# The opening of a two-layer fp32 kernel: unread products, an early table load, another order of transfers

## The chip, the cores and the metric

The kernel runs on one core of a Trainium2 chip. The metric is the time of the program on the device, in microseconds; a smaller time is better. The kernel before took 775.93 us, the median of three runs (774.78 to 776.19). The profile shows one more execution.

The engines are named as in the profile: PE (TensorE; PEld is its weight load), DVE (VectorE), ACT (ScalarE), POOL (GpSimd) and SP (SyncE, which here only issues transfers). ACT issues transfers too.

## What is computed

Two transformer layers on `x` of shape (4, 512, 256), all in fp32. Only the beginning of the first layer bears on the change:

```python
xn = _layernorm(x)                         # (x - mean) / sqrt(var + 1e-5)
x = x + _L0_attn_ref(xn, ...) + _L0_ffn_ref(xn, ...)
# inside the attention
h_in = _rmsnorm(xn, norm1_w)               # norm1_w * xn * rsqrt(mean(xn^2) + 1e-6)
v = h_in @ wv
i_pre = _soft_cap(h_in @ w_ig + b_ig)
f_pre = _soft_cap(h_in @ w_fg + b_fg)
# inside the feed-forward network
router_logits = xn @ Wr.T
```

The attention is a gated linear attention (mLSTM) with eight heads, followed by a gated MLP; the feed-forward network has eight low-rank experts of which two are chosen per token. The second layer has a softmax attention and an MLP with a 2-of-4 sparsification. The output is `x` after both layers.

## The kernel before

**Tiling.** The 512 positions are cut into four tiles `j` of 128; a tile holds the 128 positions of all four batches, as `x_sb[j]` of shape [128, 4, 256], so `b` below is one of four rows of a tile. Each tile is normalised, transposed on PE (128x128 at a time), and multiplied with the weights. All work goes out on in-order engines.

**What sets the order.** The kernel has a planner: a class `Clock` that keeps an estimated time for each engine and each buffer, and a class `Flow` that runs generators ("streams") as their due times come. The estimates decide in which order instructions are written into each engine's queue; once built, the order is fixed. So an instruction added at the front changes estimates, and can change the order later. PSUM has eight banks, all handed out by `mm_ps`; a bank whose last estimated user is PE counts as not free.

**Transfers.** They are issued by SP and ACT in program order, into SBUF tiles. At most eight were outstanding at a time in this trace: the ninth issue, on whichever of the two engines, waits until an earlier one has landed. All weights of both halves of the first layer are issued at the start, from `load_x(0)` (L342) to L382; they take until about 36 us to land.

**The opening.** `load_x(0)` fetches the four rows of the first tile in four transfers, three on SP and row 1 on ACT. Then ACT fetches the four parts of `wvg` (values, two gates, router: 256 + 8 + 8 + 8 columns), SP fetches `norm1_w` after the first of these, ACT the two gate biases. `first_front` (L528) is the first tile's front: ACT multiplies the 272 columns of `wvg` that belong to the attention by `norm1_w` (L538; the router's 8 columns stay as they are); for each row, DVE takes the statistics (`bn_stats`, `bn_aggr`), Pool adds the epsilon and takes the power -0.5, DVE normalises (`normed`, L540), PE transposes into `pt`, ACT copies into `xnT`, and PE multiplies by `wvg` into `vp` (`values`, L516). The row that is normalised is one behind the row whose statistics are taken, and the product is one behind that. After it `choice` picks the experts, while PE goes on with the low-rank products `lp`, with `q_ps`, `k_ps`, and, after `spread`, with `chunk`, the experts' products.

A matrix product of two fp32 operands takes two passes on PE, so one `mm` over 256 contracted elements shows as four records; a transpose shows as one.

Of the kernel before, what the change touches and what calls it, by code (L numbers as in the profile page):

```python
# [9 lines left out]
AF = mybir.ActivationFunctionType  # L10
ALU = mybir.AluOpType
AX = mybir.AxisListType

P = 128
B, S, D = 4, 512, 256
NJ = S // P
KD = D // P
H, DQK, DV = 8, 16, 32
# [4 lines left out]
E, R, K_TOP = 8, 16, 2  # L23
# [9 lines left out]
def layers_kernel(ctx: ExitStack, tc: tile.TileContext, io: dict, out: bass.AP):  # L33
    nc = tc.nc
    x_d = io["x"]

    const = ctx.enter_context(tc.tile_pool(name="const", bufs=1))
# [7 lines left out]
    def n_of(ap):  # L45
        n = 1
        for m in ap.shape[1:]:
            n *= m
        return n

    class Clock:
# [36 lines left out]
        def room(self, n):  # L88

            return sorted(self.bank_free(i) for i in range(BANKS))[n - 1]  # L90


        def part(self, ap):
# [86 lines left out]
        def dma(self, out, in_, us, kind="sp"):  # L180
            start = max(self.free[kind], self.ready(out, reads=True, but="dma"),
                        self.ready(in_)) + 0.5
            self.free[kind] = start
            self.free["dma"] = max(start, self.free["dma"]) + us
            end = self.free["dma"] + 2.0
            for ap, w, r in ((out, end, 0.0), (in_, 0.0, end)):
                self.known(ap.tensor.name).append((*self.part(ap), w, r, "dma"))

    clock = Clock()

    def new(pool, shape, tag, bufs=None, dtype=F32):
        count[0] += 1
        kw = {} if bufs is None else {"bufs": bufs}
        t = pool.tile(shape, dtype, tag=tag, name=f"{tag}_{count[0]}", **kw)
        clock.ring(t, (id(pool), tag), bufs or (2 if tag in ("xn", "xnT") else 1))
        return t

    def mm_ps(name):
        count[0] += 1
        t = psum.tile([P, 512], F32, tag="mm", bufs=BANKS, name=f"{name}_{count[0]}")  # L200
        clock.take_bank(t)
        return t

    class InOrder:
# [15 lines left out]
    pe, dve, act, pool = (InOrder(e, k) for e, k in (  # L220
        (nc.tensor, "pe"), (nc.vector, "dve"), (nc.scalar, "act"), (nc.gpsimd, "pool")))
# [71 lines left out]
    def mm(out, lhsT, rhs, start, stop, at_once=1, **kw):  # L293
        array = (lhsT.shape[0], n_of(lhsT))
        us = 2 * max(0.107, n_of(rhs) * 0.00084) / at_once + 0.1 * (array != clock.array)
        clock.array = array
        clock.issue("pe", "matmul", (out, lhsT, rhs), {}, us)
        pe.matmul(out, lhsT, rhs, start=start, stop=stop, **kw)

    def transpose(out, in_, eye):  # L300
        array = (in_.shape[0], n_of(in_))
        us = 0.11 + 0.1 * (array != clock.array)
        clock.array = array
        clock.issue("pe", "transpose", (out, in_, eye), {}, us)
        pe.transpose(out, in_, eye)
# [6 lines left out]
    def load(t, src, by="sp"):  # L312
        dma(t, src, n_of(t) * t.shape[0] * 4 / 0.3e6, by)
        return t
# [6 lines left out]
            "p (k n) -> p k n", n=n)  # L321
        return load(t, d.rearrange("(k p) n -> p k n", p=P), by)

    def column(name):
        t = new(const, [P, KD], name)
        return load(t, io[name].rearrange("(k p) -> p k", p=P))

    x_sb = []

    def load_x(j):  # L330

        t = new(xres, [P, B, D], f"x{j}")
        x_sb.append(t)
        src = x_d[:, j * P : (j + 1) * P, :].rearrange("b p d -> p b d")
        if j:
            load(t, src)
        else:
            for b in range(B):
                load(t[:, b, :], src[:, b, :], ("sp", "act", "sp", "sp")[b])


    load_x(0)  # L342
    V = D + 2 * H + E
    wvg = new(wts, [P, KD, V], "wvg")
    at = 0
    for name, n in (("wv", D), ("w_ig", H), ("w_fg", H), ("WrT", E)):
        load(wvg[:, :, at : at + n], io[name].rearrange("(k p) n -> p k n", p=P), "act")
        at += n
        if at == D:
            norm1_c = column("norm1_w")  # L350
    gate_b = new(const, [P, 2 * H], "gate_b")
    load(gate_b[:, 0:H], io["b_ig"].partition_broadcast(P), "act")
    load(gate_b[:, H : 2 * H], io["b_fg"].partition_broadcast(P), "act")
# [21 lines left out]
    mh_c = column("mh_w")  # L375
    w_out = weight("w_out", D)
    norm2_c = column("norm2_w")
    w_gate = weight("w_gate", FF)
    w_up = weight("w_up", FF)
    w_down = weight("w_down", D)  # L380
    for j in range(2, NJ):
# [3 lines left out]
    ident = new(const, [P, P], "ident")  # L385
# [15 lines left out]
        out=before, in_=before, pattern=[[1, E], [-1, E]], compare_op=ALU.is_gt,  # L401
# [5 lines left out]
    for base, step in ((0, -2 * DQK), (2 * DQK - 1, 2 * DQK)):  # L407
        nc.gpsimd.affine_select(
            out=own_pair, in_=own_pair, pattern=[[step, H // 2]], compare_op=ALU.is_ge,
            fill=0.0, base=base, channel_multiplier=1 if step < 0 else -1)  # L410
    def inv_sqrt(o, i):
        n = i.shape[1]
        pool.tensor_tensor(out=o, in0=i, in1=mhalf[:, 0:n], op=ALU.pow)
# [58 lines left out]
    with ExitStack() as l0:  # L472
# [8 lines left out]
        def cols_of(i):  # L481
            return slice(i * P, (i + 1) * P)
# [19 lines left out]
        def front_tiles(j):  # L502
            xns[j] = new(both, [P, B, D], "xn")

            rrs[j] = new(sm, [P, 4, B], "rr", 2)
            vas[j] = new(wk0, [P, B, H, DV + 1], "va", 2), new(sm, [P, B, 2 * H], "gz", 2)
            return xns[j], rrs[j], *vas[j], new(both, [P, KD, S], "xnT"), new(sm, [P, B, E], "pr")

        def rms_of(rr, ms, va):

            dve.tensor_tensor(rr[:, 1, :], rr[:, 0, :], rr[:, 0, :], ALU.mult)
            dve.tensor_scalar(rr[:, 2, :], rr[:, 0, :], 0.5, None, ALU.mult)
            dve.tensor_tensor(ms, ms, rr[:, 0, :], ALU.mult)
            dve.tensor_copy(va[:, :, :, DV], rr[:, 0, :].unsqueeze(2).to_broadcast([P, B, H]))

        def values(xnT, b):  # L516
            vp = mm_ps("vp")
            for k in range(KD):
                mm(vp[:, 0:V], xnT[:, k, cols_of(b)], wvg[:, k, :], start=(k == 0),
                   stop=(k == KD - 1))  # L520
            return vp

        def values_read(vp, b, rr, va, gz):
            dve.scalar_tensor_tensor(
                gz[:, b, :], vp[:, D : D + 2 * H], rr[:, 0, b : b + 1], gate_b, ALU.mult, ALU.add)
            act.mul(va[:, b, :, 0:DV], by_head(vp[:, 0:D]), rr[:, 1, b : b + 1])

        def first_front():  # L528

            x = x_sb[0]  # L530
            xn, rr, va, gz, xnT, pr = front_tiles(0)
            stats = new(both, [P, B, 6], "stats", 2)
            mv = new(both, [P, B, 2], "mv", 2)
            rstd = new(both, [P, 2, B], "rstd2")

            for k in range(KD):
                mine = wvg[:, k, 0 : D + 2 * H]
                act.mul(mine, mine, norm1_c[:, k : k + 1])  # L538

            def normed(b):  # L540
                dve.tensor_scalar(
                    xn[:, b, :], x[:, b, :], mv[:, b, 0:1], rstd[:, 1, b : b + 1], ALU.subtract,
                    ALU.mult)
                pt = mm_ps("pt")
                for k in range(KD):
                    transpose(pt[:, k * P : (k + 1) * P], xn[:, b, k * P : (k + 1) * P], ident)
                act.copy(xnT[:, :, cols_of(b)], pt[:, 0 : KD * P].rearrange(
                    "p (k t) -> p k t", k=KD))

            vps = []  # L550
            for b in range(B):
                dve.bn_stats(stats[:, b, :], x[:, b, :])
                dve.bn_aggr(mv[:, b, :], stats[:, b, :])
                pool.tensor_scalar(rstd[:, 0, b : b + 1], mv[:, b, 1:2], 1e-5, None, ALU.add)
                inv_sqrt(rstd[:, 1, b : b + 1], rstd[:, 0, b : b + 1])
                if b:
                    normed(b - 1)
                if b > 1:
                    vps.append(values(xnT, b - 2))

            ms = rr[:, 3, :]
            dve.reciprocal(ms, rstd[:, 0, :])
            dve.tensor_tensor(ms, ms, mv[:, :, 1], ALU.mult)
            dve.tensor_scalar(ms, ms, 1e-6, None, ALU.add)
            inv_sqrt(rr[:, 0, :], ms)
            normed(B - 1)
            for b in range(B - 2, B):
                vps.append(values(xnT, b))
            for w in (wq, wk, w_og):
                for k in range(KD):  # L570
                    pool.tensor_scalar(
                        w[:, k, :], w[:, k, :], norm1_c[:, k : k + 1], None, ALU.mult)
            for b in range(B):
                dve.tensor_copy(pr[:, b, :], vps[b][:, D + 2 * H : V])

            def values_of_all():
                rms_of(rr, ms, va)
                for b in range(B):
                    values_read(vps[b], b, rr, va, gz)

            xnTs[0] = xnT
            yield from choice(0, pr, values_of_all)
# [964 lines left out]
```

## Time and profile before

| What | Value |
|---|---|
| runs | 775.93 us, median of 3 (774.78 to 776.19) |
| profiled execution | 776.43 us |
| its span, first to last instruction | 774.6 us |
| PE's share of the span | 99% |
| first record of PE | 5.71 us, `pt` |
| first product with values | 8.72 us, `vp` |
| first `lp` | 16.09 us |
| granted TensorE clock | 1.0 in all 40 slices |

The page cuts the span into 40 slices of 19.4 us; the first slice is the only one with an idle PE worth the name (busy tenths, then the transfers' rate):

```
PE   6999999999999999999999999999999999999998
GB/s 253 282 97 1 1 1 1 110 ...
```

A transfer is shown from its issue; a wait is the idle time of an engine, with the instruction whose end released it. A wait that depends on several things is put down to the last of them. In the timeline, equal instructions that follow one another are drawn together, with their number after an x.

The opening as ACT saw it (start us, us, engine, line, operation, out<-in, number, idle time before and its releaser):

```profile
0.80 0.42 ACTq L309 DMA_DIRECT2D x<-in_x  x1
1.25 0.45 ACTq L309 DMA_DIRECT2D wvg<-in_wv  x1
...
3.55 0.38 ACTq L309 DMA_DIRECT2D wvg<-in_WrT  x1
4.30 0.35 ACTq L309 DMA_DIRECT2D gate_b<-in_b_ig  x1
5.73 0.35 ACTq L309 DMA_DIRECT2D gate_b<-in_b_fg  x1
6.18 1.28 ACT L216 ACT_TABLE_LOAD   x1 [6.18 <-DMA wvg<-in_WrT]
```

The issues take time on ACT's own queue, and instructions that compute stand behind them.

### The profile page before, as it was taken

How to read it: one execution, taken by the hardware profiler on the slowest of the kernel's cores; microseconds unless marked ns; L12 is line 12 of the kernel's file. 1: busy time of each engine (PE TensorE's matmuls, PEld its weight loads, DVE VectorE, ACT ScalarE, POOL GpSimd, SP SyncE). 2: the span in 40 equal slices, each digit the busy share in tenths (PEclk: the TensorE clock that was granted, in tenths of full speed). 3: DMA queues.
4: the chain of work that ended last, by engine and by line, in shares of the span. 5: the costliest groups of instructions: out<-in, count | busy, mean ns of one | idle time of the engine just before them, and what ended most of it. 6: DMA issues, size and time to landing. Idle time of an engine off the chain costs nothing.

```text
span 774.6 us, 9712 instructions
## 1 busy us (share of the span) xinstructions
PE 763.0 (99%) x3782; PEld 516.6 (67%) x3782; DVE 471.4 (61%) x1070; ACT 225.7 (29%) x457; POOL 160.6 (21%) x151
## 2 busy tenths in 40 slices
PE   6999999999999999999999999999999999999998
PEld 3677786766657776765777774747545575754487
DVE  4878647977552878634378534332366984837980
ACT  2334314332212342313134312010344305243310
POOL 5322051321230410140030041000333203333000
PEclk9999999999999999999999999999999999999999
DMA  8830000300000300000030120001000000000000
GB/s 253 282 97 1 1 1 1 110 1 1 1 1 1 110 0 1 2 0 1 1 110 1 56 96 14 1 0 55 0 1 0 0 28 1 0 28 0 0 28 29
DMA packets 18975, 25.44 MB, mean 33 GB/s; under 512 B 2800, under 2 KB 12784, under 8 KB 18928
## 3 DMA queue, kind: packets, MB, share of 16 engines
q1 hardware_dynamic: 17408, 24.39, 9.9%
q8 instruction: 30, 0.49, 0.3%
q10 hardware_dynamic: 1520, 0.43, 0.2%
q14 instruction: 17, 0.14, 0.1%
HBM read 22.65 MB, written 2.16 MB: 32 GB/s over the span
## 4 chain that ended last, share of the span: by engine, by line
PE 98%; DVE 1%; DMA 1%; ACT 0%; issue 0%
PE chunk L216 20%; PE yp L216 18%; PE up L216 14%; PE gp L216 14%; PE acc L216 11%; PE qk_ps L216 4%; PE vp L216 2%; PE pt L216 2%; PE v_ps L216 2%; PE o_ps L216 2%; PE lp L216 2%; PE qk L216 1%; PE hv L216 1%; PE sums L216 1%; PE k_ps L216 1%; PE q_ps L216 1%
## 5 line engine op out<-in xcount | busy, mean ns | idle before, releaser
L216 ACT ACTIVATE sl<-chunk 128x256 f32<-128x256 f32 x132 | 50.6, 384 | 134.5 <-PE chunk L216 118.1
L216 PE MATMUL chunk<-low,lora 128*128 128x256 f32 (+1 forms) x384 | 87.3, 385 | 0.9 <-DVE he_pair L216 0.7
L216 PE MATMUL chunk<-xnT,wguT 128*128 128x256 f32 (+1 forms) x384 | 84.5, 384 | 0.0
L216 PEld LDWEIGHTS chunk<-xnT,wguT 128*128 128x128 f32 (+1 forms) x384 | 63.6, 181 | 23.5 <-issue 11.5
L216 PEld LDWEIGHTS chunk<-low,lora 128*128 128x128 f32 (+1 forms) x384 | 63.0, 181 | 14.9 <-issue 2.1
L216 DVE SCALAR_TENSOR_TENSOR sl<-sl,chunk 128x256 f32<-128x256 f32 x132 | 54.4, 412 | 11.3 <-ACT sl L216 10.7
L216 PE MATMUL gp<-xnT,wguT 128*128 128x512 f32 x128 | 60.2, 592 | 0.0
L216 PE MATMUL up<-featT,w_up 128*128 128x512 f32 x128 | 60.2, 592 | 0.0
L216 PE MATMUL gp<-featT,w_gate 128*128 128x512 f32 x128 | 60.1, 592 | 0.0
L216 PE MATMUL up<-xnT,lora 128*128 128x512 f32 x128 | 60.1, 592 | 0.0
L216 PE MATMUL yp<-w_down,hid 128*128 128x256 f32 x256 | 56.2, 379 | 0.0
L216 PE MATMUL yp<-w_gate,hs 128*128 128x256 f32 x256 | 56.2, 379 | 0.0
L216 PEld LDWEIGHTS yp<-w_down,hid 128*128 128x128 f32 x256 | 48.5, 190 | 8.2 <-issue 1.7
L216 PEld LDWEIGHTS yp<-w_gate,hs 128*128 128x128 f32 x256 | 48.6, 190 | 6.6
L216 DVE SCALAR_TENSOR_TENSOR tmp<-tmp,gp 128x512 f32<-128x512 f32 x32 | 21.9, 685 | 42.8 <-ACT tmp L216 42.8
L216 ACT ACTIVATE tmp<-gp 128x512 f32<-128x512 f32 x32 | 19.1, 597 | 96.7 <-PE gp L216 96.7
L216 PEld LDWEIGHTS up<-xnT,lora 128*128 128x128 f32 x128 | 24.3, 190 | 29.3 <-issue 28.0
L216 PEld LDWEIGHTS up<-featT,w_up 128*128 128x128 f32 x128 | 24.1, 190 | 27.9 <-issue 26.3
L216 PEld LDWEIGHTS gp<-xnT,wguT 128*128 128x128 f32 x128 | 24.0, 190 | 27.8 <-issue 27.0
L216 PEld LDWEIGHTS gp<-featT,w_gate 128*128 128x128 f32 x128 | 24.1, 190 | 27.6 <-issue 27.3
L216 POOL TENSOR_TENSOR pd<-k,q 128x256 f32<-128x256 f32 (+3 forms) x16 | 25.3, 1583 | 81.8 <-ACT k L216 81.8
L216 PE MATMUL acc<-WdT,hid 128*128 128x256 f32 (+1 forms) x192 | 40.9, 386 | 0.0
(211 smaller groups left out, 1192.0 us busy)
## 6 DMA issues: line engine op xcount, KB each, us to landing
ct<-m_dram SPq DMA_DIRECT2D x8, 1024.0 KB, 8.1
x<-in_x SPq DMA_DIRECT2D x3, 512.0 KB, 9.6
out<-x SPq DMA_DIRECT2D x6, 256.0 KB, 2.1
w_gate<-in_w_gate SPq DMA_DIRECT2D x1, 1024.0 KB, 6.7
w_up<-in_w_up SPq DMA_DIRECT2D x1, 1024.0 KB, 7.6
w_down<-in_w_down SPq DMA_DIRECT2D x1, 1024.0 KB, 10.6
wguT<-in_f_gate SPq DMA_DIRECT2D x1, 1024.0 KB, 5.0
lora<-in_f_up SPq DMA_DIRECT2D x1, 1024.0 KB, 5.0
```

Of the source, the lines that this page charges most:

```text
L216: return tc.keep_in_program_order(f(*args, **kw))
```

## The change

- **Transfers.** The first tile comes in three transfers, all on SP: row 0, row 1, rows 2 and 3 together. `norm1_w` is ACT's first transfer, `wv`, `w_ig` and `w_fg` follow on ACT; the router's part `WrT` goes to SP.
- **Table.** A tile of one column is set to zero on DVE, and ACT takes its exponential, after its first four transfers and ahead of the two gate biases. The result is used by nothing. The number of table loads in the program stays the same.
- **Norm weight.** ACT multiplies the 256 value columns of `wvg`; the 16 gate columns of both halves are multiplied on Pool, by one product with a broadcast `norm1_w`.
- **Unread products.** PE multiplies the identity by itself nine times into a bank `idle`, and twice more after the first row's transposes. `let_go` tells the planner that the bank is free.
- **Order in `first_front`.** DVE takes the statistics of rows 0 to 2, and adds the epsilon itself; Pool takes the powers of rows 0 and 1; row 0 is normalised; then come row 3's statistics, Pool's product for the gates, one power for rows 2 and 3, and rows 1 and 2. `values` still runs one row behind.

Further on, the planner writes some instructions in another order. On PE the order is unchanged to the experts' first `acc` products with `he_pair`; from there on single groups of tiles 0 to 2 change places (the second tile's `vp` after two more groups of `chunk`, and its first `qk` directly after `vp`; `spread` of the next tile one group of `acc` later), and the second layer is unchanged. On DVE the subtraction on `ct` stands one pair of operations earlier.

```diff
@@ class Clock
+        def let_go(self, t):
+            self.known(t[:].tensor.name).append((0, 1 << 40, 0.0, self.free["pe"], ""))
@@ load_x
-            for b in range(B):
-                load(t[:, b, :], src[:, b, :], ("sp", "act", "sp", "sp")[b])
-    load_x(0)
+            for b0, b1 in ((0, 1), (1, 2), (2, 4)):
+                load(t[:, b0:b1, :], src[:, b0:b1, :])
@@ weights
-    for name, n in (("wv", D), ("w_ig", H), ("w_fg", H), ("WrT", E)):
-        load(wvg[:, :, at : at + n], io[name].rearrange("(k p) n -> p k n", p=P), "act")
-        at += n
-        if at == D:
-            norm1_c = column("norm1_w")
+    load_x(0)
+    norm1_c = column("norm1_w", "act")
+    into_wvg("wv", 0, "act")
+    into_wvg("w_ig", D, "act")
+    into_wvg("w_fg", D + H, "act")
+    into_wvg("WrT", D + 2 * H, "sp")
+    early = new(const, [P, 1], "early")
+    nc.vector.memset(early, 0.0)
+    nc.scalar.activation(early, early, AF.Exp)
@@ first_front
-                mine = wvg[:, k, 0 : D + 2 * H]
-                act.mul(mine, mine, norm1_c[:, k : k + 1])
+                act.mul(wvg[:, k, 0:D], wvg[:, k, 0:D], norm1_c[:, k : k + 1])
+            idle = mm_ps("idle")
+            def keep_busy(n):
+                for _ in range(n):
+                    mm(idle[:, 0:P], ident, ident, start=True, stop=True)
+            keep_busy(9)
@@ normed, at its end
+                if b == 0:
+                    keep_busy(2)
+                    clock.let_go(idle)
@@ first_front
-            for b in range(B):
+            def statistics(b):
                 dve.bn_stats(stats[:, b, :], x[:, b, :])
                 dve.bn_aggr(mv[:, b, :], stats[:, b, :])
-                pool.tensor_scalar(rstd[:, 0, b : b + 1], mv[:, b, 1:2], 1e-5, None, ALU.add)
+                dve.tensor_scalar(rstd[:, 0, b : b + 1], mv[:, b, 1:2], 1e-5, None, ALU.add)
+            for b in range(B - 1):
+                statistics(b)
+            for b in range(2):
                 inv_sqrt(rstd[:, 1, b : b + 1], rstd[:, 0, b : b + 1])
-                if b:
-                    normed(b - 1)
-                if b > 1:
-                    vps.append(values(xnT, b - 2))
+            normed(0)
+            statistics(B - 1)
+            gates = wvg[:, :, D : D + 2 * H]
+            pool.tensor_tensor(
+                out=gates, in0=gates, in1=norm1_c.unsqueeze(2).to_broadcast([P, KD, 2 * H]),
+                op=ALU.mult)
+            inv_sqrt(rstd[:, 1, 2:B], rstd[:, 0, 2:B])
+            for b in range(1, B - 1):
+                normed(b)
+                vps.append(values(xnT, b - 1))
```

## The prediction

> **What bounds the kernel now.** I read the page first, for the engine that sets the end, then TensorE's waits, then the chain of waits over the first 24 us.
>
> ```profile
> PE 763.0 (99%) x3782; PEld 516.6 (67%) x3782; DVE 471.4 (61%) x1070; ACT 225.7 (29%) x457; POOL 160.6 (21%) x151
> ```
> ```profile
> PE pt L216 <- DVE xn L216: 5.9, 2, 5.7
> PE vp L216 <- ACT xnT L216: 1.4, 1, 1.4
> PE chunk L216 <- DVE he_pair L216: 0.7, 1, 0.7
> PE yp L216 <- ACT oT L216: 0.2, 1, 0.2
> PE chunk L216 <- DVE tmp L216: 0.2, 1, 0.2
> ```
>
> The second view (total us, times, longest) is the whole of TensorE's idle time: 8.5 us, of which 7.3 lie ahead of 8.72 us. After that TensorE is the bound, so a microsecond saved in the opening reaches the end unless a new wait takes it. The chain of waits of the opening (start, us, what):
>
> ```profile
> 0.80 2.72 DMA x<-in_x
> ...
> 3.55 2.64 DMA wvg<-in_WrT
> 6.19 1.28 ACT L216
> ...
> 7.48 0.93 ACT wvg L216 x2
> 8.41 0.27 ACT xnT L216
> ...
> 8.72 2.23 PE vp L216 x4
> 10.96 0.43 PE pt L216 x2
> 11.38 1.87 PE vp L216 x4
> 13.25 0.43 PE pt L216 x2
> 13.68 2.58 PE vp L216 x8
> 16.25 3.43 PE lp L216 x8
> ```
>
> Two things are to be seen. ACT's table load (1.28 us, the line without a tile) and the two scalings of `wvg` stand behind ACT's own transfers, and the first product with values waits for them. And the products before about 15 us are slow: four of `vp` take 1.87 us, 0.467 each, where the chain of the whole span has for the same 16 products in the next tile
>
> ```profile
> 69.25 3.77 PE vp L216 x16
> ```
>
> that is 0.236 each. Transposes show the same halving, 0.213 against 0.109 in `spread` (0.44 for four). The page's granted clock is 1.0 in every slice, so this is another limit than the throttle that this row records. In the order of single products the step changes once, at 14.9 us, 6.1 us after unbroken work began.
>
> **The change, step by step.** Times are from the start of the span; the sum is against the profiled execution, 776.43 us, 0.5 over the median of 775.93.
>
> *Transfers.* Row 1 of `x` moves from ACT's queue to second on SP, rows 2 and 3 become one 256 KB transfer, third on SP, issued at 1.72. The 128 KB pieces took 3.0 us from issue to landing, `wv` (256 KB) 3.5, `AgT` at a busier moment 4.1: landing between 4.7 and 5.8, I take 5.3, just above `wv`'s. `norm1_w` leaves SP and `WrT` joins it, so `wq` and all behind it keep their place; the weights are needed late (`lp` took its `AgT` long landed).
>
> *Rows.* In DVE's queue the statistics of rows 0, 1 and 2 now stand ahead of the first normalised row, so `xn` of row 0 waits for the large transfer. From 5.3: statistics 0.42, aggregate 0.18, the addition that Pool did (0.25) now on DVE at 0.17 as its 128x4 neighbour, with gaps `xn` starts at 6.1, takes 0.41, and the first `pt` starts at 6.56, against 5.71: **0.85 later**. Row 3's statistics follow, `xn` of row 1 ends at 7.57, its `pt` starts at 7.63.
>
> *ACT.* Its first four transfers are out at 2.74; the table load follows at once, to about 4.0, the one-element activation to 4.3. Then `b_ig` and `b_fg`; the latter went out only at 6.07 in this trace and I leave it there. The two scalings (0.93 together) end by 7.0, the copy of the first `xnT` (0.35) by 7.4. Before, the same copy ended at 8.68. The table load is hidden behind the wait for `x`; without that cover it would cost its 1.28.
>
> *Pool.* Two powers of one column (0.58 each) end by 5.6. The 16 gate columns are a shape this trace lacks: above 0.23 (one column) and below 0.6 (`wq`, 128x128, 0.61); both ends lie between the landing of `w_fg` near 6.0 and the last power's input at 7.25, so nothing is added. The power of two columns lies between 0.58 and the 1.19 of four columns: 0.78 by the line through both, ending at 8.05; `xn` of row 2 ends at 8.5, its `pt` is due on PE at 8.78.
>
> *Values.* `pt` of row 1 takes 0.21 at full speed, so the first `vp` starts at 7.84 instead of 8.72. Then 16 products of 0.236 are 3.78, four transposes 0.43: `lp` starts at 12.05 instead of 16.09. **Gain 4.0 us**: 0.9 from the earlier start, 3.1 from the speed.
>
> *The unread products.* Nine of 128x128, two passes each at 0.213, run from `ident` (1.50) to about 5.36; nothing is behind them before 6.56. The two after the first `pt` take 0.43 at full speed or 0.85 slow, and would push the next `pt` from 7.63 to 7.84 at worst.
>
> Whether they buy the speed is the dispute. The row says 6.1 us of unbroken work were needed: 3.84 is too short, a pause of 1.2 follows, and counted from 6.56 the step would come at 12.7. The Trainium skill (TensorE: Matmul & The Clock Gate, "What's actually happening") says that the clock is halved by default and freed after one busy window of about 3.4 us that runs free of the kernel, and falls back after an idle window as long. By it 3.84 us suffice when a window fits, and a pause of 1.2 loses nothing. The same section speaks against counting on it: one kernel showed 6, 11 or 14 slow products by where the window fell. Slow throughout, `vp` starts at 8.27 and needs 16 x 0.467 + 4 x 0.213 = 8.32, to 16.6, less half of what comes after the step: by the row 14.65, by the page 12.05. I take the page: 6.1 is what one whole window costs when another had just begun at 8.72, and the three runs' spread of 1.4 us is near the 1.7 that half a window is worth. No run here shows it.
>
> *Further on.* The order from the first `acc` on is re-planned. DVE reaches the first subtraction on `ct` at 49.86 - 4.0 - 0.84 (one pair of products earlier in its queue) = 45.0, but Pool's select, which waits on a transfer behind all the weights, ends at 45.91: 0.9 us in which DVE's queue stands. The pairs behind it free banks with some 2 us to spare, so most is covered. The first `qk` now directly follows `vp` and waits for ACT's reading of its banks (0.47). Against that, the 0.7 wait for `he_pair` may go, as DVE now makes it ahead of the two additions to `xn`. The bounds are -0.7 and +1.4; I take +0.4.
>
> 776.43 - 4.04 + 0.4 = **772.8**.
>
> **Rivals.**
> *The clock is freed late.* For: the 6.1 us of the row, and that the first stretch is hardly longer than a window. Work from 6.56 is then unbroken, so the step comes between 10 and 12.7, `lp` starts at 13.3 to 14.65: 774.0 to 775.4, 774.7 in the middle.
> *Handed back.* The clock is early, but both waits above reach PE in full: 772.4 + 0.9 + 0.5, and another such wait of about 0.4: 774.2. For it: the `ct` landing doesn't move when PE does. Against: PE had no wait between 8.72 and 118 us.
> *Rows late, slower.* The statistics of row 2 hold every row. If the 256 KB land late, PE pauses over 3.4 us after its unread products, and is slow again: `lp` starts 9.3 us after landing (1.26 to `pt`, then 8.1 for slow work that speeds up 6.1 us later). It decides from a landing at 8.3, where `lp` is 1.5 later than before; at 9.8, as `w_og` (256 KB) took 8.1 us from issue, it is 19.1 and the time 779.8. Against: `w_og` stood behind two 704 KB transfers, this one behind 256 KB.
>
> **How the numbers follow.** A difference of 0.2% (1.55 us) is about what this kernel's runs can tell from no change. Early clock 0.53, late clock 0.27, handed back 0.12, late rows 0.08. Faster means under 774.4: nearly all of the first, half of the second, two thirds of the third, 0.73; no change 0.19; slower 0.08. The range goes from 771.8 (landing at 4.7, nothing handed back) to 775.4 (clock by the row).
>
> **What would show it.** Right: `vp` at 0.236 from its first product, first `vp` at 7.8, `lp` near 12, table load near 2.8, later PE waits near 1 us in all. Wrong: the step of 0.467 in several `vp`, a first `pt` well after 6.6, a PE wait near 45 or 70 us, or `ct` landing later than 43.8.

## The result, and the profile after

The changed kernel takes **774.37 us**, the median of 19 runs (772.95 to 775.32); the kernel before, run beside it, takes 775.82 (19 runs, 774.78 to 776.33). The ratio is 0.9984, 95% interval 0.9978 to 0.9991. So the gain is 1.45 us where 3.1 were predicted: the direction and the range hold, the size is just under half. The profiled execution took 774.77 us (span 773.1) against 776.43 (774.6); between these two the gain is 1.66, where the prediction's own sum, which starts from 776.43, has 3.6.

TensorE's waits after the change (us in total, times, longest), to be held against the five of before:

```profile
PE pt L220 <- DVE xn L220: 1.9, 2, 1.8
PE idle L220 <- POOL ident masks.py:199: 1.5, 1, 1.5
PE yp L220 <- ACT oT L220: 0.2, 1, 0.2
PE chunk L220 <- DVE tmp L220: 0.2, 1, 0.2
PE hv L220 <- DVE ct L220: 0.2, 1, 0.2
```

The idle time is halved, from 8.5 us to 4. The 1.4 for `xnT` and the 0.7 for `he_pair` are gone, and one new wait of 0.2 (`hv` for `ct`) has come. But 1.8 us in one piece still stand ahead of the first `pt`.

The chain of waits of the opening (start, us, what):

```profile
1.72 4.19 DMA x<-in_x
5.91 0.02 issue
5.94 0.44 DVE stats L220
...
6.77 0.36 DVE xn L220
...
8.25 0.60 PE pt L220 x2
8.85 1.93 PE vp L220 x4
10.78 0.43 PE pt L220 x2
11.21 1.30 PE vp L220 x4
12.51 0.22 PE pt L220 x2
12.73 1.89 PE vp L220 x8
14.62 3.43 PE lp L220 x8
```

ACT is gone from it: neither the table load nor a scaling stands there any more, and the 256 KB transfer of rows 2 and 3 has taken their place. Four of `vp` take 1.93 us, then four take 1.30, then eight take 1.89: the old slow step, a mixed group, the full speed. The change of speed falls at 11.8 us.

Engines by stretch of the opening (stretch, its length; busy time and instructions of PE, PEld, DVE, ACT, POOL; PEclk, DMA share, GB/s):

```profile
1.60:4.90 3.30, 3.30 (x16) 3.30 (x17) 1.62 (x7) 1.49 (x2) 1.57 (x8) 1.00 0.85 239
4.90:8.30 3.40, 1.47 (x11) 1.09 (x10) 2.12 (x8) 1.28 (x3) 1.09 (x3) 1.00 0.82 170
8.30:11.80 3.50, 3.50 (x10) 2.65 (x11) 1.31 (x6) 0.74 (x2) 2.48 (x4) 0.51 0.90 306
11.80:15.20 3.40, 3.40 (x15) 2.46 (x15) 0.81 (x6) 0.37 (x1) 2.35 (x5) 1.00 1.04 399
```

Here the profile says outright what the page's 40 slices hide. PEclk is the granted share of TensorE's full clock. The trace has clock records that begin at 4.98 (full), at 8.39 (half) and at 11.80 (full), 3.41 us apart. In the first stretch the unread products fill PE, and the clock is free at its end. In the second PE is busy for 1.47 of 3.40 us, and at its end **the clock is taken back**. In the third PE is full again, at half speed, and at its end the clock returns. Passes of 128 columns follow each other by 0.111 us in the second stretch, where the clock is free, and by 0.213 in the third.

From `lp` on nothing has moved: profiled time less the start of the first `lp` is 776.43 - 16.09 = 760.34 before and 774.77 - 14.45 = 760.32 after. The whole gain lies in the opening, and so does the whole shortfall.

This is one execution. The record has the mean granted clock of each run, and one window of 3.41 us at half speed lowers it to 0.998 over this span (1 - 3.41 x 0.5 / 773.1). Six of the 19 runs read 0.998, at 774.37 to 775.32, the median run among them. The other 13 read 0.999 or 1.000 and lost no whole window behind the first record: two of them are the fastest (772.95 and 773.06), eleven lie at 773.91 to 774.96. Time ahead of the first clock record counts as full in this mean, so a clock that is freed late leaves no mark in it. Late freeing is the likely reason for these eleven, but none of them was profiled.

### The profile page after: what moved, and what is told of

Same layout as the page of the kernel before. It is cut to its first block, busy times and chain, and to the rows that moved or that the text cites. A ratio compares the mean times of both kernels' runs of the same rounds, so it can differ in the third digit from the quotient of the medians.

```text
span 773.1 us, 9758 instructions
## 1 busy us (share of the span) xinstructions
PE 765.8 (99%) x3804; PEld 519.9 (67%) x3804; DVE 471.1 (61%) x1075; ACT 226.1 (29%) x458; POOL 158.6 (21%) x147
## 4 chain that ended last, share of the span: by engine, by line
PE 97%; DVE 1%; DMA 1%; issue 0%; SPq 0%; ACT 0%
PE chunk L220 20%; PE yp L220 18%; PE up L220 14%; PE gp L220 14%; PE acc L220 11%; PE qk_ps L220 4%; PE pt L220 2%; PE vp L220 2%; PE o_ps L220 2%; PE v_ps L220 2%; PE lp L220 2%; PE qk L220 1%; PE k_ps L220 1%; PE q_ps L220 1%; PE hv L220 1%; PE sums L220 1%
```

## The experiments

The theory after the result: the unread products do free the clock, but the pause behind them gives it back for one window of 3.41 us, which costs about 1.7 us (3.41 us of work done at half speed). Its rivals: the unread products are useless, and the gain is that of transfers and table; or the late rows alone are the trouble; or the gain is lost further on; or, in other runs than the profiled one, the clock is freed late.

Results in one table. The first three columns are those of the profiled execution: start of the first `vp`, start of the first `lp`, and the time less the latter. "Freed" is the start of the first clock record.

| Kernel | `vp` | `lp` | rest | freed | median us (runs: lowest to highest) | ratio to before (95%) |
|---|---|---|---|---|---|---|
| before | 8.72 | 16.09 | 760.34 | 14.94 | 775.92 / 775.71 / 775.86, on three chips | 1 |
| changed kernel | 8.64 | 14.45 | 760.32 | 4.98, lost 8.39 to 11.80 | 774.37 (19: 772.95 to 775.32) | 0.9984 (0.9978 to 0.9991) |
| a_no_idle | 8.46 | 13.82 | 760.51 | 10.77 | 774.82 (21: 774.03 to 775.78) | 0.9987 (0.9981 to 0.9994) |
| a_fill | 8.84 | 13.05 | 760.35 | 6.86 | 773.13 (5: 772.83 to 774.20) | 0.9965 (0.9951 to 0.9979) |
| a_split | 7.74 | 12.04 | 760.62 | 4.78 | 772.66 (5: 772.43 to 773.88) | 0.9960 (0.9947 to 0.9972) |
| **a_row01** | 7.65 | 12.15 | 760.33 | 5.06 | **772.48** (5: 772.37 to 772.58) | 0.9954 (0.9942 to 0.9967) |
| b_idle | 8.82 | 13.14 | 760.27 | 7.30 | 773.45 (13: 773.29 to 775.23) | 0.9980 (0.9972 to 0.9988) |
| b_table | 8.02 | 14.84 | 760.25 | 13.12 | 775.06 (13: 774.19 to 775.75) | 0.9992 (0.9984 to 1.0000) |
| c_both | 8.23 | 12.55 | 760.26 | 6.18 | 772.81 (5: 772.73 to 772.92) | 0.9961 (0.9948 to 0.9973) |
| c_row01_cold | 7.54 | 14.52 | 760.41 | 13.01 | 774.48 (11: 773.72 to 775.38) | 0.9984 (0.9976 to 0.9993) |
| best1 | 7.80 | 12.09 | 760.89 | 7.20 | 773.08 (5: 772.98 to 773.46) | 0.9968 (0.9956 to 0.9981) |
| best4 | 8.00 | 12.32 | 761.06 | 6.38 | 773.22 (5: 772.88 to 773.38) | 0.9968 (0.9955 to 0.9980) |
| best6 | 7.16 | 12.08 | 760.65 | 5.64 | 773.62 (7: 772.73 to 773.82) | 0.9971 (0.9959 to 0.9982) |

### Without the unread products

```diff
-            keep_busy(9)
-                if b == 0:
-                    keep_busy(2)
-                    clock.let_go(idle)
```

> The changed kernel without the eleven unread products; everything else as changed. Theory 'lost again' (the products free the clock at about 5 us, the pause ahead of the first row takes it back for one window of 3.4 us): without them TensorE is slow from its first row at about 7.2 until a whole window of work has passed, so every product with values up to 11.5 to 15 us steps 0.467, lp starts at 14.5 to 16, and the median is 774.6 to 775.6, 0.2 to 1.2 above the changed kernel's 774.4. Rival 'products useless' (the earlier table load and the order of the rows made the whole gain): median within 0.2 of 774.4.

774.82, only 0.45 more than the changed kernel: most of what the change gains (1.1 of 1.45 us) comes without a single unread product. The opening's chain shows how:

```profile
7.99 0.68 PE pt L220 x2
8.67 1.87 PE vp L220 x4
10.53 0.40 PE pt L220 x2
10.93 0.94 PE vp L220 x4
```

The step of the first `vp` is slow, and the clock comes at 10.77, in the profiled run. Unbroken work begins at 7.99 instead of 8.72, which is 0.7 of the 1.1. The runs spread over 1.75 us, as those of the kernel before do, which fits a clock that is freed at another point in each run. So the median carries the verdict and not this one profile. The rival "useless" is not refuted by this run alone: as they are placed, the unread products bring 0.45 us, inside the uncertainty of a measurement of this kernel.

### The pause filled

```diff
-            keep_busy(9)
+            keep_busy(15)
-                    keep_busy(2)
+                    keep_busy(4)
```

> The changed kernel with fifteen and four unread products instead of nine and two, so that TensorE's pause ahead of the first row shrinks from 2.0 us to about 0.6 where the clock is freed near 5 us. 'Lost again': no fallback, products with values step 0.236 from the first one, lp starts near 12.7 instead of 14.45, the median is 772.8 to 773.4; where the clock is freed late, fifteen slow products (6.4 us) end at 7.9 and delay the first row by 0.7, so single runs may be at 775. 'Products useless' or 'rows alone bind': median 774.2 to 775.

773.13. The longer run of unread products ended at 7.67 by the chain and held the first `pt` back from 7.18 to 7.50; the first `vp` is 0.2 later than in the changed kernel, and `lp` is 1.4 earlier all the same, since every `vp` runs at 0.236. So the late rows alone are not what cost most: with them just as late and more unread products, 1.24 us of the loss come back. The edit does two things, though: it fills the pause, and it makes the unbroken work longer, so that the clock is also freed early more often. It does not tell the two apart.

### Rows 2 and 3 in two transfers

```diff
-            for b0, b1 in ((0, 1), (1, 2), (2, 4)):
+            for b0, b1 in ((0, 1), (1, 2), (2, 3), (3, 4)):
```

> The changed kernel with rows 2 and 3 of the first tile as two transfers of 128 KB. If the 256 KB transfer (landed at 5.91, 4.19 from issue) is what made the rows late, the statistics of row 2 start 0.5 to 0.7 earlier, near 5.3, the first pt near 6.55, lp 0.6 earlier by that alone, median 773.6 to 774.1, and the pause of 1.3 us left may or may not take the clock back. If the landing is set by the bytes ahead of it on both queues, not by its size: start at 5.7 to 5.9, median 774.2 to 774.5.

772.66. Row 2 landed at 5.12 instead of 5.91, the first `pt` began at 6.36, and the clock that was freed at 4.78 stayed. Of the 2.41 us by which `lp` is earlier than in the changed kernel, 0.90 are the earlier first `vp` and 1.51 the speed behind it: the edit mends two things at once, and in this profile the clock is the larger. The median lies below the expected 773.6 to 774.1, which left open whether the clock would be kept. One of the five runs took 773.88, with no window lost (its mean clock reads 1.000); it was not profiled.

### Rows 0 and 1 normalised first

```diff
-            for b in range(B - 1):
-                statistics(b)
             for b in range(2):
+                statistics(b)
                 inv_sqrt(rstd[:, 1, b : b + 1], rstd[:, 0, b : b + 1])
-            normed(0)
-            statistics(B - 1)
+            for b in range(2):
+                normed(b)
+            for b in range(2, B):
+                statistics(b)
...
             for b in range(1, B - 1):
-                normed(b)
+                if b > 1:
+                    normed(b)
```

> The changed kernel with rows 0 and 1 normalised and transposed before the statistics of rows 2 and 3, so DVE's queue no longer holds them behind the large transfer. 'Rows late': the first pt starts near 5.3, right behind the unread products, the second by 6.0; the first product with values is then bound by the scaling of the value weights on ACT (ends 7.5) and starts near 7.6 instead of 8.64; the pause is now 1.5 us between the second pt and that product. Lp 0.9 to 1.1 earlier if the clock is the same as in the changed kernel, median 773.3 to 773.9. If DVE's queue doesn't bind the start of the values: median within 0.2 of 774.4.

**772.48, the lowest median of all that was run**, with all five runs within 0.21 us. The expected 773.3 to 773.9 supposed the clock of the changed kernel; here it was kept. PE's timeline (start, us, engine, line, operation, out<-in, number, idle time before and its releaser), first of the changed kernel:

```profile
1.52 3.90 PE L220 MATMUL idle<-ident 128*128 128x128 f32 x18 [1.52 <-POOL ident masks.py:199]
7.18 0.44 PE L220 MATMUL pt<-ident,xn 128*128 128x128 f32 x2 [1.76 <-DVE xn L220]
7.46 0.61 PE L220 MATMUL idle<-ident 128*128 128x128 f32 x4
8.25 0.60 PE L220 MATMUL pt<-ident,xn 128*128 128x128 f32 x2 [0.18 <-DVE xn L220]
8.64 2.14 PE L220 MATMUL vp<-wvg,xnT 128*128 128x280 f32 x4
```

and of this version:

```profile
1.52 3.95 PE L220 MATMUL idle<-ident 128*128 128x128 f32 x18 [1.52 <-POOL ident masks.py:199]
5.31 0.38 PE L220 MATMUL pt<-ident,xn 128*128 128x128 f32 x2
5.53 0.61 PE L220 MATMUL idle<-ident 128*128 128x128 f32 x4
6.11 0.44 PE L220 MATMUL pt<-ident,xn 128*128 128x128 f32 x2
7.65 1.18 PE L220 MATMUL vp<-wvg,xnT 128*128 128x280 f32 x4 [1.10 <-ACT xnT L220]
```

The unread products now run straight into the first transposes, and unbroken work lasts from 1.52 to 6.55 instead of 5.43. A pause remains (1.10 us ahead of `vp`), but the window in which it falls is still mostly busy, and the four `vp` take 1.18 us instead of 2.14:

```profile
5.00:8.40 3.40, 2.30 (x15) 1.83 (x15) 1.99 (x9) 1.44 (x4) 1.54 (x3) 1.00 0.84 172
8.40:11.80 3.40, 3.40 (x17) 2.48 (x16) 1.51 (x8) 0.75 (x2) 2.47 (x4) 1.00 0.91 290
```

A window with 2.30 of 3.40 us busy kept the clock, where one with 1.47 of 3.40 lost it.

### That version without the unread products

The edit of a_row01 and that of a_no_idle together.

> The fastest version so far (the changed kernel with rows 0 and 1 normalised first, 772.48) without the unread products; order of the other products as there. It asks what the freed clock is worth where nothing else holds the values. Theory: vp starts near 7.7 as with them, but at 0.467, the step comes one whole window after work became dense, between 10.5 and 13.5, so lp starts at 13.3 to 14.5 instead of 12.15 and the time is 773.6 to 774.8, spread over 1 us or more by where the window falls. Rival (transposes at 5.3 already start the window, so the unread products are worth little here): 772.5 to 773.0.

774.48, and 1.7 us of spread is back. In the profile `vp` starts as early as with the unread products (7.54), the clock is freed at 13.01, and `lp` starts 2.4 us later. So the same unread products that bring 0.45 us in the changed kernel bring **2.0 us** once the rows follow them without a gap. That refutes "useless".

### Unread products alone, on the kernel before

```diff
+            keep_busy(9)
...
+                if b == 0:
+                    keep_busy(2)
+                    clock.let_go(idle)
```

> The kernel before with the unread products alone: nine ahead of the first transposes and two behind them; transfers, table load, order of rows and order of products on TensorE stay as before. It asks what the unread products are worth where the loads stay. TensorE then works from 1.5 to about 5.3, pauses 0.4 or less before the first pt at 5.7 and has a pause of about 1 us before the first vp at 8.7, a shorter one than the 2.0 us that lost the clock in the changed kernel. Theory (a window of 3.4 us with over half of it busy keeps the freed clock): vp at 0.236 from 8.7 on, lp starts near 13 instead of 16.1, time 772.8 to 773.6. Rival (clock lost again in the pause): some vp at 0.467 between 8.7 and 12, lp near 14.7, 774.3 to 774.8. Rival (unread products do nothing by themselves, the gain comes from loads and table): 775.6 to 776.2.

Ratio 0.9980: about what the whole change gains, with the transfers, the table load and the order of all other products as they were. The single runs fall into two groups that are 1.7 us apart: seven at 773.29 to 773.45, six at 774.78 to 775.23, with nothing between. The profiled run (773.41) belongs to the first, and kept its clock through a pause of 1.32 us:

```profile
8.82 1.21 PE L220 MATMUL vp<-wvg,xnT 128*128 128x280 f32 x4 [1.32 <-ACT xnT L220]
```

The mean granted clock of the single runs separates the groups without an exception: 1.000 in all seven of the first, 0.998 in all six of the second. So the second group did lose the clock for about one window, and 1.7 us is what the loss costs. This is the theory shown in 13 runs, where the profile of the changed kernel showed it in one. All 13 had the clock early, kept or lost; PE worked without a gap from 1.52 to 7.50 in the profiled one, the transposes included. In the changed kernel such work ends at 5.43, and only eight of 19 runs bear a sign of an early clock: the six at 0.998 and the two at 772.95 and 773.06, which lie apart from the other 17.

### The early table load alone, on the kernel before

```diff
+    early = new(const, [P, 1], "early")
+    nc.vector.memset(early, 0.0)
+    nc.scalar.activation(early, early, AF.Exp)
```

> The kernel before with the early table load alone (zero tile on DVE and one-element Exp on ACT ahead of the two bias loads). No unread products, rows and transfers as before. Theory (the run without unread products gained 1.1 of the 1.5 us, and the table load of 1.28 us stood in the chain of the opening right ahead of the scalings): the scalings end about 1.2 us earlier, the first vp starts near 7.5 instead of 8.7, the products stay slow at first, lp starts 0.6 to 1.3 us earlier: 774.5 to 775.3. Rival (the moved transfers and the order of the rows carry that gain, or b_fg and the load of WrT on ACT's queue still hold the scalings): 775.6 to 776.2 with the scalings at 7.4 to 7.5 as before.

775.06, 0.65 less than before; the interval touches 1, so it is just at what can be told. ACT's timeline shows the load moved, not to 2.73, where ACT's fourth issue ends, but to 3.90, since it stands behind a fifth issue that is held:

```profile
3.50 0.37 ACTq L309 DMA_DIRECT2D wvg<-in_WrT  x1
3.90 1.28 ACT L353 ACT_TABLE_LOAD   x1 [3.90 <-DMA x<-in_x]
5.20 0.20 ACT L353 ACTIVATE early<-early 128x1 f32<-128x1 f32 x1
5.84 0.35 ACTq L309 DMA_DIRECT2D gate_b<-in_b_ig  x1
6.23 0.45 ACTq L309 DMA_DIRECT2D gate_b<-in_b_fg  x1
6.78 0.93 ACT L216 ACTIVATE wvg<-wvg,norm_w 128x272 f32<-128x272 f32 x2 [1.38 <-DMA wk<-in_wk]
```

Of the 1.28 us, 0.70 are saved (the first `vp` at 8.02), because the bias loads now come behind the table load and hold the scalings to 6.78. Clock freed at 13.12.

### Both of these, on the kernel before

> The kernel before with the unread products and the early table load, and nothing else of the change: transfers, rows, and the order of products on TensorE as before. Alone they gave 2.3 and 0.65 us. Theory (the two are separate terms of the sum, a start 0.8 earlier and about 3 us of speed): first vp at 8.0, all vp at 0.236 since the pause is shorter than in the run with unread products alone, lp near 12.5, 772.4 to 772.9, which is faster than the whole change (774.4). Rival (they do not add, the later work takes the earlier start back): 773.2 to 773.7.

772.81, and all five runs within 0.2 us. The gain is 3.05, where the single ones add to 2.33 (the first group of b_idle, around 773.38) + 0.65 = 2.98: in this kernel they add like separate terms. Two of the change's five parts, alone, do 1.56 us better than the whole change. Taken with a_row01, the other three parts (transfers, order of rows, gates apart) cost 1.56 us with the order as changed, and gain 0.33 with rows 0 and 1 first; the second figure lies inside the intervals.

### Three tries to add to it

best1 puts a_split and a_row01 together. best4 adds ACT's scalings ahead of the two bias loads, a power for row 2 alone, and two and four unread products behind the first two transposes. best6 is best1 with the scalings moved, and nothing else.

```diff
     nc.scalar.activation(early, early, AF.Exp)
+    for k in range(KD):
+        act.mul(wvg[:, k, 0:D], wvg[:, k, 0:D], norm1_c[:, k : k + 1])
```

> The changed kernel with both single edits of the first four runs together: rows 2 and 3 of x as two transfers, and rows 0 and 1 normalised ahead of the statistics of rows 2 and 3. If each edit gains only by keeping the clock (theory), there is nothing left for the second to add: the first vp is held by ACT's scaling of wvg (about 7.5) in both, so vp at 7.6 to 7.7, lp near 12.0, 772.2 to 772.6. Rival (the gains add, since the split brings the later rows forward too): 771.2 or less. The planner orders some later products differently here, so a loss from that order, up to 774, is the third case.

> As the last one, with ACT's scaling of the value weights ahead of the two bias loads, row 2's power taken alone, and the unread products behind the first two transposes as two and four. Theory (with the clock kept, what sets the first vp is ACT: the scaling held by b_fg's issue, which waited for the landing of w_ig): the scaling ends near 6.2 instead of 7.5, first vp near 6.6 to 6.8, lp near 11.1 to 11.5, 771.3 to 771.9. Rival (rows 2 and 3 take the place of the scaling as what binds, or a later wait such as hv on ct or the copy of row 3 takes it back): 772.3 to 772.8, as rows 0 and 1 first alone. Rival (the re-planned later order costs more than the opening saves): 773 or more.

> Rows 0 and 1 first, rows 2 and 3 as two transfers, and ACT's scaling of the value weights ahead of the two bias loads; unlike the last try, the gate product stays ahead of row 2's power in Pool's queue. In that try Pool's gate product ended at 7.96 and took the place of the scaling as what held the first vp. Theory: the scaling ends near 6.2, the gate product near 7.0, first vp at 7.1 to 7.3, lp near 11.6, 771.7 to 772.2 if the later order costs nothing. Rival (the planner's other later order, 72 rows of TensorE's listing against the fastest version's, costs what the two earlier tries lost, about 0.5): 772.3 to 773.2.

None reaches a_row01's 772.48, and each is slower than its theory had expected (772.2 to 772.6, 771.3 to 771.9, 771.7 to 772.2). best1's opening went as the theory has it, with nothing to add (7.80 and 12.09). In the other two, another engine took the place of the one relieved. In best4 it was Pool: its gate product stands behind row 2's power and ends at 7.95, the first `vp` follows at 8.00.

```profile
7.19 0.55 POOL L220 TENSOR_TENSOR rstd<-rstd,mhalf 128x1 f32<-128x1 f32 x1 [1.27 <-DVE rstd L220]
7.71 0.24 POOL L220 TENSOR_TENSOR wvg<-wvg,norm_w 128x32 f32<-128x32 f32 x1
```

In best6 the first `vp` does start early, at 7.16, but row 2 then holds PE at 8.75, and `lp` starts at 12.08, hardly before the 12.15 of a_row01. And behind `lp` each loses 0.3 to 0.7 us (760.65 to 761.06 in the table, against 760.33). best4's waits show where it may lie:

```profile
PE chunk L220 <- DVE hid L220: 0.7, 2, 0.5
PE chunk L220 <- DVE he_pair L220: 0.7, 1, 0.7
```

Neither is in the changed kernel or in a_row01. The wait for `he_pair` alone is no proof of a loss, since the kernel before has it too, with a rest of 760.34; and a_split has a rest of 760.62 without any such wait, so 0.3 us is not told from chance. The planner writes later products in another order when its estimates of the opening change; that this order is the cause was not tested by itself. Six of best6's seven runs lie 0.6 to 1.1 us above its profiled one. They lost no window (their mean clock reads 1.000); why they are slower stays open.

## Why the prediction was right in direction and half right in size

Term by term, by the prediction's own sum:

- **The landing of rows 2 and 3** was taken at 5.3 (bounds 4.7 and 5.8) and measured 5.91, outside the upper bound. From there on the working held: `xn` 0.77 after it against 0.8, `pt` 1.27 after it against 1.26. First `pt` 7.18 instead of 6.56.
- **ACT.** The table load ran at 2.85, early as said, hidden behind the wait for `x`. The scalings ended at 7.51 instead of 7.0, since the issue of `b_fg` on ACT's own queue, which the prediction had left at 6.07, ended at 6.50. Here this costs nothing, as the second `pt` came at 8.25; in a_row01 it is what holds `vp`.
- **Pool.** The gates took 0.24, the two-column power 0.80: 0.24 lies at the low bound, 0.80 at the 0.78 of the line. Both hidden, as said.
- **First `vp`** 8.64 instead of 7.84, 0.8 late: 0.6 by the landing, 0.2 because the two of the second `pt`, in whose midst the clock was halved, took 0.39 and not 0.21.
- **Speed.** From the first `vp` to `lp` 4.21 us were predicted and 5.81 taken. **This is the step that failed: "3.84 us suffice when a window fits, and a pause of 1.2 loses nothing."** In the profiled run a window fitted, but the pause before the first `pt` was 1.76 us and not 1.2, because of the landing, and the clock record that begins at 8.39 shows the loss: half speed for one window, 1.6 us. Nor was a pause of 1.2 safe: b_idle's was 1.32 in its profile, and six of its 13 runs lost a window (the pause of those six was not profiled). In the eleven runs of the changed kernel that were slow without a lost window, the first half of the sentence is the likely failure: no window fitted into 3.84 us.
- **Further on**, +0.4 was taken and 0.0 measured (760.34 to 760.32). The wait for `he_pair` went, as allowed for, and the one for `ct` came, near 85 us and small.
- **A reading.** The 8.5 us were not the whole of PE's idle time: 774.6 less 763.0 is 11.6, and the other 3.1 lie behind its last product. The sum does not use them.

0.8 + 1.6 - 0.4 = 2.0 is the distance of the profiled 774.77 from 772.8; the median lies 0.4 lower.

The weighing of rule and row came out between the two. The Trainium skill (TensorE: Matmul & The Clock Gate, "What's actually happening") was right about the way in for the profiled run: unbroken work from 1.52 freed the clock at 4.98, 3.46 us later, and the row's 6.1 us before the change were one window lost and one window worked, for before the change the window ahead of the one that freed it was 82% busy. On the way out the page names an idle window of about 3.4 us, and read as a wholly idle one this fails here: a window with PE busy for 43% of it was enough. Of the rivals, "the clock is freed late" came near the size (774.7). It is not what the profiled run did, but its range of 774.0 to 775.4 holds ten of the eleven runs at 773.91 to 774.96 that lost no window, and it may be what they did. "Rows late, slower" had the mechanism of the profiled run, a late landing and a pause that costs the clock, but asked for a pause of 3.4 us, and 1.76 was enough. "Handed back" did not occur. The median fell into the predicted range because that range reached up to the late clock.

## What to carry to other kernels

Work that is there to free TensorE's clock is worth its price only if it lasts long enough to fill a window wherever the window falls, and runs into the real work. Ask not only whether the clock is freed but how full the next window is. In this kernel the same eleven products gained 0.45 us with a pause of 1.8 us behind them, and 2.0 us where the first transposes followed without a gap. A statistic or load hoisted ahead of the first product in an in-order queue makes the first result wait for the last arrival; take the rows that have landed first. When a change has several parts, run them alone: here two parts without the others gained twice as much as all together.

## What the runs showed of the hardware

- **How full a window must be.** The windows are 3.41 us long (records 4.98, 8.39, 11.80; the long records of full clock in all profiles, 761.17, 764.59 and 768.00 us, are 223, 224 and 225 times 3.4133). Counted backward and forward from the first record of each profile, with PE's busy time in each: the clock was not freed after windows that were 82% (before), 75% (c_row01_cold) and 71% busy (b_table), and it was after 89% (a_no_idle) and more. A freed clock was kept through windows 61% (b_idle), 65% (a_split), 66% (c_both), 68% (a_row01) and 72% busy (best6), and lost after one of 43% (the changed kernel). So the bar for keeping lies below the one for freeing. The two rows nearest to the bars, of a_no_idle and of b_idle, engines by stretch as above:

```profile
7.30:10.70 3.40, 3.02 (x10) 2.10 (x9) 1.86 (x9) 0.74 (x2) 2.01 (x3) 1.00 0.77 176
7.30:10.70 3.40, 2.08 (x11) 1.56 (x10) 1.28 (x6) 2.10 (x6) 3.17 (x6) 1.00 0.88 234
```

The windows without a record of their own are placed by calculation, and where between 43% and 61% the lower bar lies was not tried. Nor do these runs tell the busy share of a window from its longest pause, which was 1.76 us where the clock was lost and 1.32 at most where it was kept.
- **How long the work must be.** This is an estimate from the figures above. If a window counts when it is 82 to 89% full, work of 3.84 us holds one in 34 to 48% of all positions of the windows; eight of the changed kernel's 19 runs, 42%, bear a sign of an early clock. Twice 82 to 89% of 3.41, that is 5.6 to 6.1 us without a gap, would hold one in every position; b_idle had 6.0, and all its 13 runs had the clock early.
- **The window does not start with the kernel.** In profiles of kernels that all begin their unread products at 1.52, the clock was freed at 4.78, 4.98, 5.06, 5.64, 6.18, 6.38, 6.86, 7.20 and 7.30, over 2.5 us. That fits the spread of a kernel whose opening leaves the clock to chance (775.92: 774.76 to 776.50, and half a window is 1.7 us), and the 0.2 us of a_row01 and c_both, which have five runs each. Five runs are too few to say that these two keep the clock wherever the windows fall.
- **A clock of 1.00 in a row can mean "no record".** The kernel before, at half speed (0.467 a `vp`), engines by stretch as above:

```profile
8.10:11.50 3.40, 2.78 (x7) 2.15 (x8) 0.66 (x3) 0.93 (x4) 3.26 (x6) 1.00 0.84 230
```

The clock column reads 1.00 there, for the trace has no clock record ahead of 14.94. The duration of a known instruction is the better witness; the prediction had read the page's 1.0 as a sign of "another limit than the throttle". The changed kernel's row shows the same 0.467 a `vp` where the recorded clock is 0.51, so it is the same limit.
- **One transfer of 256 KB, or two of 128.** Third on SP and issued at 1.72, the 256 KB landed after 4.19 us; row 2 alone, at the same place and time, after 3.40 (a_split). Here the first half's reader paid 0.8 us for the second; that is one profile of each.
